# A selective-scan kernel: single PSUM banks for the decays, delta loaded one unit ahead, side stages at half the rate

## The chip, the cores and the metric

The kernel runs on one core of a Trainium2 chip. The metric is the device time in microseconds, the median of several runs of the whole program; lower is better. One further execution was recorded by the hardware profiler, and all views below are of it.

## What is computed

Four layers on an image batch `x` of shape (4, 64, 64, 96). Layers 2 and 3 are linear attention and a small quantised feed-forward network; the change does not touch them. Layers 0 and 1 are 2D selective scans ("SS2D"). Their core, cut:

```python
xz = einsum('bhwc,ec->bhwe', x, in_proj_w);  xx, z = split(xz, 2)         # 96 -> 2 x 192 channels
xc = silu(depthwise_conv3x3(xx) + conv_b)
xs = stack([x_hw, x_wh, x_hw[..., ::-1], x_wh[..., ::-1]])                # 4 directions k, L = 4096 steps
dts, Bmat, Cmat = split(einsum('bkdl,kcd->bkcl', xs, x_proj_weight), ...)  # 6, 16, 16 rows
delta = softplus(einsum('bkrl,kdr->bkdl', dts, dt_projs_weight) + bias)
h = exp(delta * A) * h + delta * B * u                                    # per step, state of 16 per channel
y = einsum('bken,bkn->bke', h, C)                                         # + D * u, directions added up
out = out_proj(layernorm(y) * silu(z))
```

## The kernel before, in words

The batch is cut into two pairs of images, and layers 0 and 1 give four *phases* (layer, pair), run one after the other. In a phase 8 groups (4 directions × 2 images) × 16 states fill the 128 partitions. The 4096 steps are cut into 8 chunks of 512, the 192 channels into 16 blocks of 12. A chunk and a block make a *unit*: 128 units a phase, 512 in all.

For each unit:
- `load` (L321) issues on SP's queue four loads of `dlt` (delta, 8 partitions each at 0, 32, 64 and 96) and four of `h` (delta·u, 8 groups spread over 128 partitions, 768 KB each). `h` has four buffers, `dlt` two.
- `times_b` (L339): four multiplications `h = h·b` on POOL.
- `scan` (L345), six times a unit (*slots*). A slot takes two channels: two replication matmuls on PE (L353, 8 rows of delta to 128 partitions, in the row group of that channel) into a tile `a` of two PSUM banks, two exponentials on ACT in place (L356), two scans on DVE (L360), which read `a` and overwrite `h`. The pool `p_a` has two such tiles, four banks. After the last slot ACT copies the final states to `carry` (L370).
- `contract` (L372), four times a unit, for the unit before: 32 small matmuls with the weights `cw` on PE (L381) into one bank of `p_y` (two banks), a copy to `d` on ACT (L391); after the fourth, four stores `y<-d` (L402). The weights are made on POOL once a chunk (`weights`, L301).

*Side stages* are generators whose `yield`s cut them into small steps. `prepare` (L131) makes `delta`, `du` and `bc` of the next phase: statistics, two convolutions (L228, one bank per chunk, nine matmuls and a silu), and `steps` (L250): per direction and chunk two x_proj matmuls (L257), a copy `xd` (L260), two dt_w matmuls (L267), two softplus (L273), a product on DVE (L276), and three stores. `finish` (L406) turns `y` of the phase before into the layer's output. They take PSUM banks from `bank()`, a pool `p_bg` of two.

The loop `run` (L557) mixes all this. For unit `at`, slot `n`, it calls `scan`, in slots 0 to 3 `contract` of unit `at-1`, in slot 4 `fetch` of unit `at+3` (loads and `times_b`), and then advances the side stages by `rate` 1.5 steps: nine a unit. When three units are left before the next phase, what is left of the side stages is run out. Before the first unit `prepare` of phase 0 runs alone; after the last, `finish` of phase 3; then layers 2 and 3.

The order of each engine's queue is settled at build time by a scheduler that starts from this program order and may move instructions by priority and by when it believes their inputs to be ready. All DMAs go through SP's queue in order; a DMA also waits until the one eight places ahead of it in that queue has landed.

Of the kernel before, what the change touches and what calls it, by code (L numbers as in the profile page):

```python
# [9 lines left out]
F32 = mybir.dt.float32  # L10
F16 = mybir.dt.float16
FP8 = mybir.dt.float8e5
AF = mybir.ActivationFunctionType
ALU = mybir.AluOpType
PSUM = bass.MemoryType.PSUM
# [6 lines left out]
C = 96  # L22
# [4 lines left out]
G = 2 * K  # L27
PAD = HW + 2
TC = 512
NC = L // TC  # L30
ROWS = TC // HW
EB = 12
NEB = E // EB
ER = EB // 4
XD = 2 * NS + R + 1
HID = 384
NF = HID // 128
EPS = 1e-5
LN_EXP = "natural_log_exp_and_others"
SQRT_HALF = 0.7071067811865476  # L40

# [33 lines left out]
class Consts:  # L75
    def __init__(self, nc, pool, a):
# [14 lines left out]
        self.eps = pool.tile([128, 1], F32, name="eps")  # L91
        nc.vector.memset(self.eps, EPS)


def neg_rsqrt(nc, cst, var, ln, r, sq):
# [3 lines left out]
    nc.scalar.activation(sq, r, AF.Square, scale=SQRT_HALF)  # L99
    nc.vector.scalar_tensor_tensor(sq, var, EPS, sq, ALU.add, ALU.mult)  # L100
    nc.vector.scalar_tensor_tensor(r, sq, 1.5, r, ALU.subtract, ALU.mult)
# [9 lines left out]
class Scans:  # L111
    def __init__(self, tc, ctx, cst, a):
        nc = self.nc = tc.nc
        self.tc, self.cst, self.a = tc, cst, a

        def pool(name, bufs, **space):
            return ctx.enter_context(tc.tile_pool(name=name, bufs=bufs, **space))

        self.dram = pool("stage", 2, space=DRAM)
        self.keep = pool("keep", 2)  # L120
        self.units = pool("units", 2)
        self.p_a = pool("p_a", 2, space=PSUM)
        self.p_y = pool("p_y", 2, space=PSUM)
        self.p_bg = pool("p_bg", 2, space=PSUM)

    def bank(self):
        return self.p_bg.tile([128, TC], F32, name="bg")

# [119 lines left out]
    def steps(self, ph, sp, xc, xp, dt_w, i, k, c):  # L250

        nc, cst = self.nc, self.cst
        g = 2 * k + i
        u = scan_view(xc, k, c)
        ps = self.bank()
        for h in range(2):
            nc.tensor.matmul(rows(ps[:XD]), xp[:, k, h], u[:, h], start=h == 0, stop=h == 1)  # L257
        xd = sp.tile([XD, TC], F32, name="xd")

        nc.scalar.activation(xd, ps[:XD], AF.Identity, bias=cst.one_row)  # L260
        yield
        nc.sync.dma_start(ph.bc[c][g], xd[: 2 * NS])
        delta = sp.tile([C, 2, TC], F32, name="dl")
        raw = []
        for m in range(2):
            ps = self.bank()
            nc.tensor.matmul(  # L267
                ps[:C], dt_w[2 * NS :, k, m * C : (m + 1) * C], xd[2 * NS :], start=True, stop=True
            )
            raw.append(ps)  # L270
        yield
        for m in range(2):
            nc.scalar.activation(delta[:, m], raw[m][:C], AF.Softplus)  # L273
        yield
        du = sp.tile([C, 2, TC], F32, name="du_sb")
        nc.vector.tensor_tensor(rows(du), rows(delta), u, ALU.mult)  # L276
        nc.sync.dma_start(ph.delta[c][g].rearrange("(h q) t -> q h t", h=2), delta)
        yield
        nc.sync.dma_start(ph.du[c][g].rearrange("(h q) t -> q h t", h=2), du)
# [37 lines left out]
    class Unit:  # L317
        def __init__(self, ph, c, eb):
            self.ph, self.c, self.eb = ph, c, eb

    def load(self, u):  # L321

        nc, ph = self.nc, u.ph
        h, v = divmod(u.eb, NEB // 2)
        u.first = [h * C + r * (C // 4) + ER * v for r in range(4)]
        u.dl = self.units.tile([128, ER, TC], F32, name="dlt")
        u.h = self.units.tile([128, EB, TC], F32, name="h", bufs=4)
        for r, at in enumerate(u.first):
            nc.sync.dma_start(u.dl[32 * r : 32 * r + G], ph.delta[u.c][:, at : at + ER])
        for r, at in enumerate(u.first):  # L330
            nc.sync.dma_start(
                u.h[:, ER * r : ER * r + ER].rearrange("p e t -> p (e t)"),
                ph.du[u.c][:, at : at + ER]
                .rearrange("g e t -> g (e t)")
                .unsqueeze(1)
                .broadcast_to([G, NS, ER * TC]),
            )
# [4 lines left out]
            h = u.h[:, ER * r : ER * r + ER]  # L342
            self.nc.gpsimd.tensor_tensor(h, h, b, ALU.mult)  # L343

    def scan(self, u, n):  # L345

        nc, ph = self.nc, u.ph
        half, i = divmod(n, ER)
        a = self.p_a.tile([128, 2, TC], F32, name="a")
        for j in range(2):  # L350
            r = 2 * half + j
            part = slice(32 * r, 32 * r + G)
            nc.tensor.matmul(a[:, j], self.cst.rep[part], u.dl[part, i], start=True, stop=True)  # L353
        for j in range(2):
            at = u.first[2 * half + j] + i
            nc.scalar.activation(a[:, j], a[:, j], AF.Exp, scale=ph.a_col[:, at : at + 1])  # L356
        for j in range(2):
            e = ER * (2 * half + j) + i
            at = u.eb * EB + e
            nc.vector.tensor_tensor_scan(  # L360
                u.h[:, e],
                a[:, j],
                u.h[:, e],
                0.0 if u.c == 0 else ph.carry[:, at : at + 1],
                ALU.mult,
                ALU.add,
            )
        if n == EB // 2 - 1 and u.c < NC - 1:
            at = u.eb * EB
            nc.scalar.copy(ph.carry[:, at : at + EB], u.h[:, :, TC - 1])  # L370

    def contract(self, u, l1):  # L372

        nc, ph = self.nc, u.ph
        y = self.p_y.tile([128, TC], F32, name="y_ps")
        for l2 in range(8):
            for j in range(4):  # L380
                nc.tensor.matmul(  # L381
                    view(y[32 * j : 32 * j + 32], l2 * EB, (8 * EB, 4), (1, EB)),
                    u.cw[l1][:, 8 * j + l2],
                    view(u.h, 64 * l1 + 16 * j + l2, (256, 2), (8, 2), (TC, EB)),
                    start=True,
                    stop=True,
                )
        if l1 == 0:

            u.d = self.units.tile([128, 4, 2, 4, 4 * EB], F32, name="d")  # L390
        nc.scalar.copy(  # L391
            u.d[:, :, :, l1], y[:, : 32 * EB].rearrange("p (t h x) -> p t h x", t=4, h=2)
        )
        if l1 < 3:
            return
        for t in range(4):
            b, m = divmod(t, 2)

            dst = ph.y[:, u.c * 8 : u.c * 8 + 8, u.eb, b].rearrange(
                "g (j m) h x -> m j g (h x)", m=2  # L400
            )[m]
            nc.sync.dma_start(dst, u.d[t::4, t].rearrange("p h l x -> p (h l x)"))  # L402
# [154 lines left out]
    def run(self, phases):  # L557

        def behind(p):
            if p > 0:
                yield from self.finish(phases[p - 1])
            if p + 1 < len(phases):
                yield from self.prepare(phases[p + 1])

        units = [
            self.Unit(ph, c, eb) for ph in phases for c in range(NC) for eb in range(NEB)
        ]
        per = NC * NEB  # L570
        slots = EB // 2

        def fetch(u):
            if u.eb == 0:
                self.start_chunk(u.ph, u.c)
            self.load(u)
            self.times_b(u)

        for _ in self.prepare(phases[0]):
            pass  # L580
        for u in units[:3]:
            fetch(u)
        self.weights(units[0].ph)
        rate = 1.5
        due = 0.0
        rest = iter(())
        for at, u in enumerate(units):
            for n in range(slots):
                self.scan(u, n)
                if n == 0:  # L590
                    u.cw = u.ph.cw if u.eb or at == 0 else None
                if at and n < 4:
                    self.contract(units[at - 1], n)
                if n == 4:
                    if at and u.eb == 0:
                        self.weights(u.ph)
                        u.cw = u.ph.cw
                    if at % per == 0:
                        rest = behind(at // per)
                        due = 0.0  # L600
                    if at + 3 < len(units):
                        if (at + 3) % per == 0:
                            for _ in rest:
                                pass
                        fetch(units[at + 3])
                due += rate
                while due >= 1.0:
                    next(rest, None)
                    due -= 1.0
        for q in range(4):  # L610
            self.contract(units[-1], q)
        for _ in self.finish(phases[-1]):
            pass

# [233 lines left out]
```

## Time and profile before

| | us |
|---|---|
| median of 3 runs (18317.12 to 18345.54) | 18334.98 |
| the profiled execution | 18288.92 |
| its span | 18287.0 |
| before the first scan (`prepare` of phase 0) | 852 |
| scans, four phases | 15494 |
| after the last scan (`finish` of phase 3) | 424 |
| layers 2 and 3 | 1517 |

| engine, over the span | busy us | share |
|---|---|---|
| PE (matmul) | 13227.8 | 72% |
| DVE | 9175.7 | 50% |
| POOL | 7455.9 | 41% |
| ACT | 7427.5 | 41% |

The four phases last 3771, 4095, 4091 and 3538 us. In the profile a row of a group gives busy time, mean duration and the idle time ahead of it with what ended it; `h<-du` reads "tile h, from du", and `xN` is a count. A fp32 matmul is two instructions in the trace.

### The profile page before, as it was taken

The numbers are of one execution on the slowest core, as the hardware profiler recorded it, in microseconds if no ns is written. First come the engines' busy times: TensorE is split into PE (matmuls) and PEld (weight loads), VectorE is DVE, ScalarE is ACT, GpSimd is POOL, SyncE is SP. The second block draws the span as 40 slices with busy tenths as digits, with TensorE's granted clock in tenths as the row PEclk, the third lists the DMA queues.
The fourth block names the chain that finished last, engine by engine and source line by source line (L and its number), as shares of the span: only waits on it lengthen the run. The fifth ranks groups of instructions, "written<-read, shape, count | busy, mean of one in ns | idle before, by whom it ended". The sixth has DMA issues, their size and how long they took to land. (4 is left out here: it accounts for less than half of the span.)

```text
span 18287.0 us, 356175 instructions
## 1 busy us (share of the span) xinstructions
PE 13227.8 (72%) x155712; PEld 6559.2 (36%) x155712; DVE 9175.7 (50%) x8726; ACT 7427.5 (41%) x12019; POOL 7455.9 (41%) x2572
## 2 busy tenths in 40 slices
PE   7887876666787897666787887666786666666555
PEld 2233333333453333333453333333453333335222
DVE  1144455555454545555454545555555555552333
ACT  2244443333333544333333544333334333342555
POOL 0034355555333435555333434555435555540000
PEclk6676666666667676666667676666666666666666
DMA  3345454444443545444443544444444444442000
GB/s 83 85 121 147 128 157 145 144 149 147 136 131 105 159 132 155 145 143 150 135 127 107 159 132 149 147 147 151 133 134 143 140 148 144 144 135 59 7 7 7
DMA packets 865414, 2293.37 MB, mean 125 GB/s; under 512 B 240854, under 2 KB 441688, under 8 KB 863476
## 3 DMA queue, kind: packets, MB, share of 16 engines
q1 hardware_dynamic: 863860, 2270.58, 42.2%
q8 instruction: 1228, 20.12, 0.5%
q14 instruction: 326, 2.67, 0.0%
HBM read 1907.51 MB, written 362.81 MB: 124 GB/s over the span
## 5 line engine op out<-in xcount | busy, mean ns | idle before, releaser
L343 POOL TENSOR_TENSOR h<-h,b 128x1536 f32<-128x1536 f32 x2048 | 7111.7, 3476 | 7564.1 <-DMA h<-du 6435.2
L360 DVE TENSOR_TENSOR_SCAN h<-a,carry,h 128x512 f32<-128x512 f32 x5376 | 6540.8, 1267 | 5372.2 <-ACT a L356 4189.9
L353 PE MATMUL a<-dlt,rep 8*128 8x512 f32 x12288 | 5474.3, 944 | 3072.7 <-DVE h L360 3054.1
L356 ACT ACTIVATE a<-a,a_col 128x512 f32<-128x512 f32 x6144 | 4013.6, 661 | 4628.3 <-PE a L353 4527.3
L381 PEld LDWEIGHTS y_ps<-h,cw 128*32 128x32 f32 x131072 | 2917.4, 146 | 3042.2 <-issue 2322.6
L381 PE MATMUL y_ps<-h,cw 128*32 128x48 f32 x131072 | 3274.1, 267 | 702.5 <-issue 353.2
L353 PEld LDWEIGHTS a<-dlt,rep 8*128 8x128 f32 x12288 | 1428.9, 258 | 4863.8 <-DVE h L360 4445.4
L391 ACT COPY d<-y_ps 128x384 f32<-128x384 f32 x2048 | 938.0, 481 | 1476.1 <-PE y_ps L381 1256.1
L360 DVE TENSOR_TENSOR_SCAN h<-a,h 128x512 f32<-128x512 f32 x768 | 892.2, 1208 | 1125.6 <-ACT a L356 705.3
L228 PE MATMUL bg<-xc,taps 96*96 96x512 f32 x2304 | 1013.4, 603 | 69.7 <-DVE xc L214 59.7
L267 PE MATMUL bg<-xd,dt_w 7*96 7x512 f32 x1024 | 859.9, 985 | 158.5 <-ACT xd L260 158.2
L276 DVE TENSOR_TENSOR du_sb<-dl,xc 96x1024 f32<-96x1024 f32 x256 | 473.7, 1850 | 878.0 <-ACT dl L273 869.2
L257 PE MATMUL bg<-xc,x_proj 96*39 96x512 f32 x1024 | 893.8, 1018 | 1.6 <-ACT dl L273 1.6
L309 POOL TENSOR_TENSOR cw<-c,gmask 128x256 f32<-128x256 f32 x512 | 323.8, 687 | 1345.2 <-DMA c<-bc 669.3
L454 PE MATMUL bg<-yk,perm 128*128 128x192 f32 x2048 | 623.4, 454 | 86.0 <-DMA yk<-y 85.6
L228 PEld LDWEIGHTS bg<-xc,taps 96*96 96x96 f32 x2304 | 380.3, 166 | 702.1 <-issue 649.2
L674 POOL MEMSET tn<- 1x4096 f32 x8 | 28.3, 3542 | 1409.3 <-PE pa L715 1386.1
L370 ACT COPY carry<-h 128x12 f32<-128x12 f32 x448 | 94.3, 210 | 1191.9 <-DVE h L360 998.3
L454 PEld LDWEIGHTS bg<-yk,perm 128*128 128x128 f32 x2048 | 473.4, 264 | 258.7 <-issue 144.8
L267 PEld LDWEIGHTS bg<-xd,dt_w 7*96 7x96 f32 x1024 | 224.1, 245 | 639.5 <-ACT xd L260 376.6
L260 ACT ACTIVATE xd<-bg,one_row 39x512 f32<-39x512 f32 x256 | 174.6, 682 | 575.3 <-PE bg L257 487.6
L235 ACT ACTIVATE xc<-bg,conv_b 96x512 f32<-96x512 f32 x128 | 87.2, 682 | 785.8 <-PE bg L228 785.8
(108 smaller groups left out, 6478.1 us busy)
## 6 DMA issues: line engine op xcount, KB each, us to landing
h<-du SPq DMA_DIRECT2D x2048, 768.0 KB
delta<-dl SPq DMA_DIRECT2D x256, 384.0 KB
du<-du_sb SPq DMA_DIRECT2D x256, 384.0 KB
dlt<-delta SPq DMA_DIRECT2D x2048, 48.0 KB
y<-d SPq DMA_DIRECT2D x2048, 48.0 KB
yk<-y SPq DMA_DIRECT2D x256, 384.0 KB
ud<-xu SPq DMA_DIRECT2D x128, 192.0 KB
ud_f<-ud SPq DMA_DIRECT2D x128, 192.0 KB
```

What stands on the lines that cost most here:

```text
L228: nc.tensor.matmul(rows(ps[:C]), taps[:, tap, h * C : (h + 1) * C], xn[:, ROWS * c + dy : ROWS * (c + 1) + dy, dx : dx + HW], start=tap == ...
L257: nc.tensor.matmul(rows(ps[:XD]), xp[:, k, h], u[:, h], start=h == 0, stop=h == 1)
L267: nc.tensor.matmul(ps[:C], dt_w[2 * NS :, k, m * C : (m + 1) * C], xd[2 * NS :], start=True, stop=True)
L276: nc.vector.tensor_tensor(rows(du), rows(delta), u, ALU.mult)
L309: self.nc.gpsimd.tensor_tensor(view(cw, t, (256, 4), (32, 8), (4, G)), view(ph.c_next, 256 * b + 64 * l1 + 8 * m, (16, 4), (1, 8), (0, G)) ...
L343: self.nc.gpsimd.tensor_tensor(h, h, b, ALU.mult)
L353: nc.tensor.matmul(a[:, j], self.cst.rep[part], u.dl[part, i], start=True, stop=True)
L356: nc.scalar.activation(a[:, j], a[:, j], AF.Exp, scale=ph.a_col[:, at : at + 1])
L360: nc.vector.tensor_tensor_scan(u.h[:, e], a[:, j], u.h[:, e], 0.0 if u.c == 0 else ph.carry[:, at : at + 1], ALU.mult, ALU.add,)
L381: nc.tensor.matmul(view(y[32 * j : 32 * j + 32], l2 * EB, (8 * EB, 4), (1, EB)), u.cw[l1][:, 8 * j + l2], view(u.h, 64 * l1 + 16 * j + l2, ...
L391: nc.scalar.copy(u.d[:, :, :, l1], y[:, : 32 * EB].rearrange("p (t h x) -> p t h x", t=4, h=2))
L454: nc.tensor.matmul(ps[:, : 4 * n].rearrange("p (w v e) -> p w v e", w=4, v=nv), cst.perm[:, k], view(t, off, (sw if k < 2 else -sw, 4), (1 ...
```

## The change

Four things:
1. The pools. `p_a` becomes six single banks, one decay (one channel) each. `p_y` and `p_bg` become one pool `p_m` of two banks, which contraction and side stages share. Outside the scans `bank()` takes from the six.
2. `scan` takes four channels (one of each row group) at a time: four replications, four exponentials, four scans; three times a unit in place of six.
3. The loads of `dlt` leave `load` for `load_delta`, called for unit `at+1` after the first step of unit `at`. `contract` is called twice in each of the first two steps, `fetch` in the second.
4. RATE stays 1.5 per step of the loop, which has three steps a unit: 4.5 side steps a unit. `steps` has a softplus right after each dt_w matmul and a `yield` after each.

```diff
-        self.p_a = pool("p_a", 2, space=PSUM)
-        self.p_y = pool("p_y", 2, space=PSUM)
-        self.p_bg = pool("p_bg", 2, space=PSUM)
+        self.p_a = pool("p_a", 6, space=PSUM)
+        self.p_m = pool("p_m", 2, space=PSUM)
+        self.scanning = False
     def bank(self):
-        return self.p_bg.tile([128, TC], F32, name="bg")
+        if self.scanning:
+            return self.p_m.tile([128, TC], F32, name="m")
+        return self.p_a.tile([128, TC], F32, name="a")
...
         for m in range(2):
             ps = self.bank()
             nc.tensor.matmul(ps[:C], dt_w[...], xd[2 * NS :], start=True, stop=True)
-            raw.append(ps)
-        yield
-        for m in range(2):
-            nc.scalar.activation(delta[:, m], raw[m][:C], AF.Softplus)
-        yield
+            nc.scalar.activation(delta[:, m], ps[:C], AF.Softplus)
+            yield
...
+    def load_delta(self, u):
+        nc, ph = self.nc, u.ph
         u.dl = self.units.tile([128, ER, TC], F32, name="dlt")
         for r, at in enumerate(u.first):
             nc.sync.dma_start(u.dl[32 * r : 32 * r + G], ph.delta[u.c][:, at : at + ER])
...
-    def scan(self, u, n):
-        half, i = divmod(n, ER)
-        a = self.p_a.tile([128, 2, TC], F32, name="a")
-        for j in range(2):
-            r = 2 * half + j
+    def scan(self, u, i):
+        decay = []
+        for r in range(4):
+            a = self.p_a.tile([128, TC], F32, name="a")
             part = slice(32 * r, 32 * r + G)
-            nc.tensor.matmul(a[:, j], self.cst.rep[part], u.dl[part, i], start=True, stop=True)
+            nc.tensor.matmul(a, self.cst.rep[part], u.dl[part, i], start=True, stop=True)
+            decay.append(a)
...
-        y = self.p_y.tile([128, TC], F32, name="y_ps")
+        y = self.p_m.tile([128, TC], F32, name="m")
...
-            for n in range(slots):
-                self.scan(u, n)
-                if n == 0:
-                    u.cw = u.ph.cw if u.eb or at == 0 else None
-                if at and n < 4:
-                    self.contract(units[at - 1], n)
-                if n == 4:
+            for i in range(ER):
+                self.scan(u, i)
+                if i == 0 and at + 1 < len(units):
+                    self.load_delta(units[at + 1])
+                if at and i < 2:
+                    self.contract(units[at - 1], 2 * i)
+                    self.contract(units[at - 1], 2 * i + 1)
+                if i == 1:
...
                         fetch(units[at + 3])
-                due += rate
+                due += RATE
```

More of the change, by code (lines that the diff above doesn't have):

```diff
@@ L38 @@
 EPS = 1e-5
+RATE = 1.5
 LN_EXP = "natural_log_exp_and_others"
@@ L263, in steps @@
         delta = sp.tile([C, 2, TC], F32, name="dl")
-        raw = []
         for m in range(2):
@@ L319, in __init__ @@
             self.ph, self.c, self.eb = ph, c, eb
+            h, v = divmod(eb, NEB // 2)
+            self.first = [h * C + r * (C // 4) + ER * v for r in range(4)]
+    def load_delta(self, u):
+        nc, ph = self.nc, u.ph
+        u.dl = self.units.tile([128, ER, TC], F32, name="dlt")
+        for r, at in enumerate(u.first):
+            nc.sync.dma_start(u.dl[32 * r : 32 * r + G], ph.delta[u.c][:, at : at + ER])
     def load(self, u):
         nc, ph = self.nc, u.ph
-        h, v = divmod(u.eb, NEB // 2)
-        u.first = [h * C + r * (C // 4) + ER * v for r in range(4)]
-        u.dl = self.units.tile([128, ER, TC], F32, name="dlt")
         u.h = self.units.tile([128, EB, TC], F32, name="h", bufs=4)
-        for r, at in enumerate(u.first):
-            nc.sync.dma_start(u.dl[32 * r : 32 * r + G], ph.delta[u.c][:, at : at + ER])
         for r, at in enumerate(u.first):
@@ L343, in times_b @@
             self.nc.gpsimd.tensor_tensor(h, h, b, ALU.mult)
-    def scan(self, u, n):
+    def scan(self, u, i):
         nc, ph = self.nc, u.ph
-        half, i = divmod(n, ER)
-        a = self.p_a.tile([128, 2, TC], F32, name="a")
-        for j in range(2):
-            r = 2 * half + j
+        decay = []
+        for r in range(4):
+            a = self.p_a.tile([128, TC], F32, name="a")
             part = slice(32 * r, 32 * r + G)
[L353 to L358, printed above, removed]
+            nc.tensor.matmul(a, self.cst.rep[part], u.dl[part, i], start=True, stop=True)
+            decay.append(a)
+        for r, a in enumerate(decay):
+            at = u.first[r] + i
+            nc.scalar.activation(a, a, AF.Exp, scale=ph.a_col[:, at : at + 1])
+        for r, a in enumerate(decay):
+            e = ER * r + i
             at = u.eb * EB + e
@@ L361, in scan @@
                 u.h[:, e],
-                a[:, j],
+                a,
                 u.h[:, e],
@@ L367, in scan @@
             )
-        if n == EB // 2 - 1 and u.c < NC - 1:
+        if i == ER - 1 and u.c < NC - 1:
             at = u.eb * EB
@@ L570, in run @@
         per = NC * NEB
-        slots = EB // 2
         def fetch(u):
@@ L582, in run @@
             fetch(u)
+        self.load_delta(units[0])
         self.weights(units[0].ph)
-        rate = 1.5
+        self.scanning = True
+        rest = iter(())
         due = 0.0
-        rest = iter(())
         for at, u in enumerate(units):
-            for n in range(slots):
-                self.scan(u, n)
-                if n == 0:
-                    u.cw = u.ph.cw if u.eb or at == 0 else None
-                if at and n < 4:
-                    self.contract(units[at - 1], n)
-                if n == 4:
+            if u.eb or at == 0:
+                u.cw = u.ph.cw
+            for i in range(ER):
[6 more added lines that the diff above has]
+                if i == 1:
                     if at and u.eb == 0:
@@ L599, in run @@
                         rest = behind(at // per)
-                        due = 0.0
                     if at + 3 < len(units):
@@ L611, in run @@
             self.contract(units[-1], q)
+        self.scanning = False
         for _ in self.finish(phases[-1]):
```

## The prediction

> **What bounds the kernel now.** I read the page first (busy shares, slices), then the stretches by stage, then the waits and the order of time inside one unit. A unit is 12 scans on DVE; 512 units follow each other in four phases of 128. The row of stretches, restricted to the scan line L360, gives the pace:
>
> ```profile
> 4623.00:7135.00 2512.00, 927.13 (x768) 0.68 0.47 134
> 7135.00:8718.00 1583.00, 932.35 (x769) 0.62 0.48 147
> ```
>
> Both halves of phase 1 hold 768 scans, 64 units. The first, with side work (`finish` of the phase before, `prepare` of the next), takes 2512/64 = 39.3 us a unit, the second, without any, 1583/64 = 24.7 us. The same stretches over all engines:
>
> ```profile
> 4623.00:7135.00 2512.00, 2024.46 (x20488) 1011.46 (x20488) 1224.49 (x1162) 1078.51 (x1681) 943.19 (x321) 0.68 0.47 134
> 7135.00:8718.00 1583.00, 1060.39 (x17920) 542.39 (x17920) 932.35 (x769) 613.90 (x1072) 918.94 (x321) 0.62 0.48 147
> ```
>
> With side work PE is busy 2024 of 2512 us (81%): PE bound. Without it PE, DVE and POOL are all near 60%, and the waits of the free half name the transfer:
>
> ```profile
> POOL h L343 <- DMA h<-du: 550.8, 215, 8.6
> ```
>
> In the order of time POOL's four multiplications of a unit each start when a piece of `h` lands:
>
> ```profile
> 7804.04 3.42 POOL L343 TENSOR_TENSOR h<-h,b 128x1536 f32<-128x1536 f32 x1 [6.74 <-DMA h<-du]
> ...
> 7810.13 3.47 POOL L343 TENSOR_TENSOR h<-h,b 128x1536 f32<-128x1536 f32 x1 [2.67 <-DMA h<-du]
> ...
> 7816.32 3.42 POOL L343 TENSOR_TENSOR h<-h,b 128x1536 f32<-128x1536 f32 x1 [2.72 <-DMA h<-du]
> ```
>
> A piece every 6.1 us; four pieces are the 24.7 us. So a free unit is bound by its 3 MB of `h`, a unit with side work by PE.
>
> [...] the share stays at 0.48 of 16, 7.7 engines, in every free stretch, so the transfer is saturated though it looks half idle. [...]
>
> ```profile
> 7809.77 2.08 PE L353 MATMUL a<-dlt,rep 8*128 8x512 f32 x4
> ...
> 7811.78 1.62 PE L381 MATMUL y_ps<-h,cw 128*32 128x48 f32 x64
> ...
> 7815.80 3.25 PE L353 MATMUL a<-dlt,rep 8*128 8x512 f32 x8 [2.40 <-DVE h L360]
> ```
>
> Each replication is two instructions: a pair takes 2.08 us and the contraction behind it starts 2.01 us after it. [...] The trace shows the 1283, and the activation 1.29 us after the load began[...]. I use 1.28.
>
> **The change part by part.**
>
> *Delta one unit ahead.* The load of `dlt` for three units ahead waits in SP's queue until the replications two units before it are through (L329, 16.67 us across its four issues at 7803.94), with the `h` loads behind it. That wait goes. But the transfer is saturated, so what is late next is the same 3 MB: worth 0 to 0.6 us a unit; I take 0. Same DMAs, same number.
>
> *Single banks.* A scan starts after one exponential instead of two: in the trace exponentials start at 7801.82 and the scan at 7803.21, 1.39 us; one exponential is 0.66 us. It shortens the ring, which isn't what bounds a free unit.
>
> *The order on PE.* This decides, and the diff doesn't show it. In the built order of before, each unit has its four contraction groups placed between replications, so they run while DVE scans. In the built order of after, a free unit is: contraction of unit u (first one waits for DVE, the last scan of u), then the replications of u+1: one alone ahead of the last contraction matmul, three, two, then six that each wait for a scan, then the contraction of u+1. So four replications are rarely side by side, and contraction and scans take turns. A free unit on this chain: 4 × 1.61 (contraction) + 2.0 (lone replication) + 2.1 (the next) + 0.66 (exponential) + 0.3 (handing over) + 11 × 1.21 (the scans left; four take 4.81) = 24.4 us. Beside it the transfer has 24.7. Two limits this close: I take 25.2. 147 such units × 0.5 = +74 us.
>
> *Side stages spread.* The steps due fall from 9 to 4.5 a unit. `finish` has 200 steps, the statistics 11, the two convolutions 80, the projections (`steps`) 256: 547 in phases 1 and 2, 347 in phase 0, 200 in phase 3. Divided by 4.5 that is 44.4, 2.4, 17.8 and 56.9 units. The total work is the same, so it gains only if it runs beside the scans. PE has about six scans of free time, 7.3 us, after a unit's last replication; but in the order of after most projection work stands behind the contraction that waits for the last scan.
> - Projections: 3.5 us of L257 and 3.4 of L267 a step (893.8/256 and 859.9/256), × 1.125 steps = 7.7 us a unit, of which the order puts some 1.7 ahead of the contraction. Up to the fourth replication: 6.4 + 6.0 + three lone replications at 2.0 + 2.1 = 20.5; exponential 0.7; nine scans left 10.9; in most units a softplus stands between exponentials, 1.28 + 0.59 + 1.28 = 3.2. That is 35.3; dt_w beside a replication (they use different rows, and overlap at 2326 us) takes about 1 off, waits not listed may add as much. I take 35, bounds 31 and 38.
> - `finish`: 16 groups of 4 × 0.61 + 4 × 0.335 = 3.8 us and two slices of 14 us per quarter. Two groups fit under the scans; the shared pair of banks allows no more, since the copy of `carry`, which waits for the last scan, is ahead of their evacuation on ACT. A unit full of groups: 15 + 2.9 + 6.4 + 18 − 7.5 = 34.8; slices (4.3 us of PE a unit): about 27. Weighted 20 to 30: 30 us, bounds 28 and 33.
> - Convolutions: 16 chunks of 7.9 us per half, 4.5 to a unit: 3.55 units of about 55, the rest near 27: 338 us per half. Statistics 26 a unit.
>
> *Table loads.* Softplus is now one per step: the order has 1208 loads against 823, +385 × 1.28 = 494 us of ACT, not all on the path; what is, stands in the 3.2 above.
>
> *Shared pair of banks* for contraction and side work: PE waits for copies of 0.48; inside the above, 0 to 1 us a unit.
>
> *Outside the phases*, `bank()` has six banks: PE is busy 703 of 852 us before the scans and 325 of 424 after; I take −40 us (0 to −100).
>
> Sum. Phases 1 and 2: 44.4 × 30 + 62 + 676 + 56.9 × 35 + 6.5 × 25.2 = 4226 each, against 4095: +131. Phase 0: 62 + 676 + 1992 + 50.9 × 25.2 = 4013 against 3771: +242. Phase 3: 1332 + 83.6 × 25.2 = 3439 against 3538: −99. Together +405, less 40: +365. The profiled execution is 18288.9 us (span 18287.0), so 18654; the median of the runs is 46 higher: 18700.
>
> **The rivals.**
> - *Side work disappears under the transfer* (faster). For it: PE would need only 16.6 + 8.2 us in a unit of the first half now spread over two, DVE 15. Then a unit with side work costs 24.7 plus its own DMA, some 29 us: phases 3684 twice, 3531, 3330, a sum of 14229 against 15495, 17070 in all. Halfway (projections 31, `finish` 28) it is 17750. Against: the order above.
> - *The turns cost more* (slower still): softplus twice in a unit's scans[...]: 39 and 33 us, + 171 × 4 + 133 × 3 = +1083: 19780. It would decide as soon as the projections pass 37 us a unit.
> - *It cancels*: projections at 33, with the rest as above: 171 × 2 = 342 less, 18360.
> - *The change doesn't act*: four replications don't stand together in the order, and the lead of `dlt` is hidden by the saturated transfer; that part is likely, and only the spreading acts.
>
> **How the numbers follow.** Turns as summed 0.57, turns costing more 0.18, cancelling 0.06, side work hidden at least half 0.19. A measurement of this kernel can tell about 0.2% (37 us). Slower 0.75, same 0.06, faster 0.19. The range takes the bounds of projections and `finish` (171 × −4 and 133 × −2 one way, 171 × 3 and 133 × 3 the other, not all at once): 18100 to 19400.
>
> **What would show it.** In the profile after: free stretches near 25 us a unit (about 1600 us for 64); DVE idle ahead of its scans for some 10 us at a time, once a unit, and L384 waiting for DVE; projections at 35 a unit; about 1208 table loads; the wait of POOL for `h` shorter in side stretches. Wrong it would be if units with side work run at 29 to 31 us with the DMA share at 0.48 or above throughout: then the order doesn't bind and the transfer does.

## The result, and the profile after

The changed kernel takes 18553.58 us (median of 4 runs, 18520.44 to 18619.85), the kernel before 18326.05 in the same session: a ratio of 1.013, with a 95% interval from 1.0098 to 1.0161. It is slower by 1.3%. The profiled execution has a span of 18518.7 us, 231.7 more than before.

The page of the changed kernel, its groups of instructions (busy time, mean ns of one, idle time ahead of the engine and what ended it; the lines have moved: the scan is L363 now, the contraction L384, the multiplication by b L346):

```profile
PE 13016.6 (70%) x155712; PEld 6734.7 (36%) x155712; DVE 9278.6 (50%) x8726; ACT 7835.8 (42%) x12404; POOL 7465.1 (40%) x2572
...
L346 POOL TENSOR_TENSOR h<-h,b 128x1536 f32<-128x1536 f32 x2048 | 7121.1, 3479 | 8143.3 <-DMA h<-du 6610.6
L363 DVE TENSOR_TENSOR_SCAN h<-a,carry,h 128x512 f32<-128x512 f32 x5376 | 6461.6, 1263 | 5041.0 <-issue 2599.0
...
L384 PE MATMUL m<-h,cw 128*32 128x48 f32 x131072 | 3281.9, 267 | 2291.1 <-issue 983.8
...
L457 PE MATMUL m<-yk,perm 128*128 128x192 f32 x1536 | 421.2, 417 | 825.5 <-DMA yk<-y 823.4
```

The rows of the scan and of the first matmul of `finish` in the kernel before:

```profile
L360 DVE TENSOR_TENSOR_SCAN h<-a,carry,h 128x512 f32<-128x512 f32 x5376 | 6540.8, 1267 | 5372.2 <-ACT a L356 4189.9
L454 PE MATMUL bg<-yk,perm 128*128 128x192 f32 x2048 | 623.4, 454 | 86.0 <-DMA yk<-y 85.6
```

The work is the same (the last `finish` has a row of its own now, hence 1536 for 2048); what differs is the waiting. Before, the idle time of the scans ended mostly with an exponential (4189.9 us of 5372.2). Now its largest part has the releaser "issue": the scan had nothing left to wait for that the profile shows, and the order of time below shows what stands ahead of it. The other new number is the 823.4 us in which PE stands at the first matmul of `finish` for `yk`, which was 85.6.

Three stretches, restricted to the scan line (start and end, length, DVE busy and number of scans, granted clock, DMA share, GB/s): `finish` and projections of phase 1, the free units of phase 3.

```profile
4641.00:6126.00 1485.00, 624.84 (x528) 0.68 0.46 132
6564.00:7447.00 883.00, 405.75 (x336) 0.63 0.48 149
14504.00:16612.00 2108.00, 1202.42 (x1008) 0.62 0.48 142
```

With 12 scans a unit these are 33.8 us for a unit with `finish`, 31.5 with projections, 25.1 free. The phases last 3721, 4175, 4154 and 3642 us (before 3771, 4095, 4091, 3538): −50, +80, +63 and +104. Up to the first scan pass 920 us (852), after the last 1907 (1941). The sum, 197 + 68 − 34, is the 231.

One free unit in the order of time (start, duration, engine, line, and in brackets the idle time ahead with its releaser):

```profile
15200.88 2.46 PE L384 MATMUL m<-h,cw 128*32 128x48 f32 x103 [0.16 <-issue]
...
15203.27 1.12 PE L355 MATMUL a<-dlt,rep 8*128 8x512 f32 x2
...
15204.59 10.01 PE L355 MATMUL a<-dlt,rep 8*128 8x512 f32 x22
...
15205.18 14.35 DVE L363 TENSOR_TENSOR_SCAN h<-a,carry,h 128x512 f32<-128x512 f32 x12 [8.16 <-issue]
...
15219.67 3.02 PE L384 MATMUL m<-h,cw 128*32 128x48 f32 x127 [5.07 <-DVE h L363]
```

The contraction of one unit, one replication, all the others, twelve scans in one run, and only then the next contraction, which waited 5.07 us for the last of them. DVE had been idle 8.16 us ahead of its run. Contraction and scans take turns, as the built order had it.

### The profile page after: what moved, and what is told of

Its sections match the earlier page's. It is cut to its first block, busy times and chain, and to the rows that moved or that the text cites. A ratio compares the mean times of both kernels' runs of the same rounds, so it can differ in the third digit from the quotient of the medians.

```text
span 18518.7 us, 353643 instructions
## 1 busy us (share of the span) xinstructions
PE 13016.6 (70%) x155712; PEld 6734.7 (36%) x155712; DVE 9278.6 (50%) x8726; ACT 7835.8 (42%) x12404; POOL 7465.1 (40%) x2572
## 3 DMA queue, kind: packets, MB, share of 16 engines
HBM read 1907.51 MB, written 362.81 MB: 123 GB/s over the span
## 5 line engine op out<-in xcount | busy, mean ns | idle before, releaser
L346 POOL TENSOR_TENSOR h<-h,b 128x1536 f32<-128x1536 f32 x2048 | 7121.1, 3479 | 8143.3 <-DMA h<-du 6610.6
L363 DVE TENSOR_TENSOR_SCAN h<-a,carry,h 128x512 f32<-128x512 f32 x5376 | 6461.6, 1263 | 5041.0 <-issue 2599.0
L384 PE MATMUL m<-h,cw 128*32 128x48 f32 x131072 | 3281.9, 267 | 2291.1 <-issue 983.8
L384 PEld LDWEIGHTS m<-h,cw 128*32 128x32 f32 x131072 | 2939.0, 140 | 3864.1 <-issue 3043.2
L355 PEld LDWEIGHTS a<-dlt,rep 8*128 8x128 f32 x12288 | 1814.5, 250 | 3273.6 <-DVE h L363 1892.3
L394 ACT COPY d<-m 128x384 f32<-128x384 f32 x2048 | 983.3, 484 | 2058.5 <-PE m L384 1891.3
L363 DVE TENSOR_TENSOR_SCAN h<-a,h 128x512 f32<-128x512 f32 x768 | 878.8, 1203 | 1148.7 <-issue 753.2
L457 PE MATMUL m<-yk,perm 128*128 128x192 f32 x1536 | 421.2, 417 | 825.5 <-DMA yk<-y 823.4
L231 PE MATMUL m<-xc,taps 96*96 96x512 f32 x1728 | 789.4, 615 | 103.4 <-issue 67.1
L457 PEld LDWEIGHTS m<-yk,perm 128*128 128x128 f32 x1536 | 311.5, 237 | 947.1 <-issue 667.5
L269 PE MATMUL m<-xd,dt_w 7*96 7x512 f32 x768 | 559.4, 835 | 127.6 <-ACT xd L263 98.9
L260 PE MATMUL m<-xc,x_proj 96*39 96x512 f32 x768 | 594.6, 894 | 0.3 <-issue 0.2
L359 ACT ACT_TABLE_LOAD x431 | 553.0, 1283 | 55.3 <-PE a L355 47.7
L231 PEld LDWEIGHTS m<-xc,taps 96*96 96x96 f32 x1728 | 285.5, 168 | 595.7 <-issue 526.4
L272 ACT ACT_TABLE_LOAD x301 | 386.2, 1283 | 8.9 <-DMA delta<-dl 3.7
```

The source lines that it names most:

```text
L231: nc.tensor.matmul(rows(ps[:C]), taps[:, tap, h * C : (h + 1) * C], xn[:, ROWS * c + dy : ROWS * (c + 1) + dy, dx : dx + HW], start=tap == ...
L269: nc.tensor.matmul(ps[:C], dt_w[2 * NS :, k, m * C : (m + 1) * C], xd[2 * NS :], start=True, stop=True)
L272: nc.scalar.activation(delta[:, m], ps[:C], AF.Softplus)
L355: nc.tensor.matmul(a, self.cst.rep[part], u.dl[part, i], start=True, stop=True)
L359: nc.scalar.activation(a, a, AF.Exp, scale=ph.a_col[:, at : at + 1])
L363: nc.vector.tensor_tensor_scan(u.h[:, e], a, u.h[:, e], 0.0 if u.c == 0 else ph.carry[:, at : at + 1], ALU.mult, ALU.add,)
```

## The experiments

All times are medians; the ratio is to the kernel before in the same session (18314.76 us for the first four, 18254.04 for the next four, 18297.65 and 18282.34 later), with its 95% interval.

| kernel | us | ratio | table loads on ACT |
|---|---|---|---|
| before | 18254 to 18326, by session | 1 | 823 |
| changed kernel | 18554 | 1.013 (1.0098 to 1.0161) | 1208 |
| 1: changed, delta loaded in `fetch` | 18167 | 0.9912 (0.9889 to 0.9936) | 873 |
| 2: before, delta one unit ahead | 19753 | 1.0779 (1.0759 to 1.0799) | 866 |
| 3: before, rate 0.75 | 18240 | 0.9962 (0.995 to 0.9973) | 919 |
| 4: changed, rate 3 | 18504 | 1.0092 (1.0059 to 1.0124) | 930 |
| 5: before, `h` on 16 engines | 21088 | 1.1551 (1.1534 to 1.1568) | |
| 6: changed, `h` on 16 engines | 22473 | 1.2307 (1.2288 to 1.2325) | |
| 7: changed, softplus in pairs | 18301 | 1.0036 (1.0009 to 1.0063) | 1156 |
| 8: 1 with `h` on 16 engines | 21863 | 1.1976 (1.1958 to 1.1994) | |
| 9: before, two copies of `du` | 18421 | 1.0073 (1.0054 to 1.0093) | 817 |
| 10: 1 and 7 together | 18151 | 0.9929 (0.9906 to 0.9952) | 857 |
| 11: before, padded rows of `du` | 18270 | 0.9988 (0.9973 to 1.0002) | |
| 12: 10 with two copies of `du` | 17529 | 0.9591 (0.9573 to 0.961) | 857 |

### 1 and 2: the lead of delta

Run 1 takes the lead of `dlt` out of the changed kernel: it is loaded in `fetch` again, ahead of `h`, three units before its use.

```diff
         def fetch(u):
...
+            self.load_delta(u)
             self.load(u)
...
-        self.load_delta(units[0])
...
-                if i == 0 and at + 1 < len(units):
-                    self.load_delta(units[at + 1])
```

> The changed kernel with the delta load put back beside the h load, three units ahead (two buffers, so its wait for the replications is back). In the built order the contraction of a unit then stands ahead of the fourth replication of the next in 0 to 0.5 of its matmuls instead of 0.3 to 1.0. Theory A, PE's order makes contraction and scans take turns: side units fall from about 32 to 28-30 us, free units stay at 24.5, in all 17900 to 18200. Theory B, the 8-engine transfer of h sets all units: no change, 18450 to 18600. Theory C, what costs is PE standing at L457 for the yk loads: no change either, the yk waits stay near 820 us.

Run 2 does that part alone: the kernel before, where after the first scan call of a unit the `dlt` of the next is loaded.

```diff
-    def load(self, u):
+    def load_delta(self, u):
...
+        self.load_delta(units[0])
...
+                if n == 0 and at + 1 < len(units):
+                    self.load_delta(units[at + 1])
```

> The kernel before with the delta load alone moved, one unit ahead after slot 0. In the built order the contraction's share ahead of the fourth replication rises from 0.25 to 0.5-0.94. Theory A: slower than before, free units 25 to 26.5 us, side units 40 to 43, in all 18500 to 18800. Theory B: the same or up to 0.5% faster, since SP is no longer held at the delta load, 18230 to 18340. Theory C: as before, 18330.

The lead alone costs 1438 us, far more than the 500 expected; without it the changed kernel is 387 us faster (18167 against 18554), and faster than the kernel before, inside theory A's time. The order on PE says why. Counted in the traces, the share of a unit's contraction that runs ahead of the fourth replication of the next unit is, in free units, 0.25 in the kernel before, 0.95 with the lead alone, 1 in the changed kernel and 0.5 in run 1. In the changed kernel it is also 1 in most units with projections, but 0.13 (median) in those with `finish` of phase 1: the turns stand in the free units and in those with projections. The edit moves only the place of the load in the program; that the scheduler then believes the replications ready at another time is the explanation that fits, and wasn't looked into. The waits of the scans over the whole program (us, times, longest), first the changed kernel:

```profile
DVE h L363 <- issue: 3352.2, 314, 43.4
DVE h L363 <- ACT a L359: 2151.7, 827, 52.1
...
DVE h L363 <- POOL h L346: 582.9, 74, 23.6
```

then run 1:

```profile
DVE h L363 <- POOL h L346: 3798.2, 915, 30.0
DVE h L363 <- ACT a L359: 2562.4, 507, 141.5
...
DVE h L363 <- issue: 185.9, 52, 13.3
...
PE m L457 <- DMA yk<-y: 56.7, 36, 3.8
```

The turns are gone ("issue" falls from 3352 to 186, PE's wait for `yk` from 823 to 57), and the `h` that POOL delivers takes their place: 583 to 3798. So a unit with projections falls from 31.1 to 27.8 us on average, while one with `finish` (34.3 for 33.8) and a free one (24.9 to 25.2 for 23.9 to 25.1) gain nothing: there the next wait lies just behind the one removed. In run 2 the turns are there without the four replications in a row, and a free unit takes 28.4 to 28.9 us where it took 24.5 to 25.2:

```profile
DVE h L363 <- issue: 3993.0, 393, 24.1
...
PE y_ps L384 <- DVE h L363: 1694.5, 433, 11.0
```

A rival is that `dlt` itself arrives too late for the replications when it is loaded so late. The waits of the replications for that DMA, in the changed kernel and in run 2, speak against it:

```profile
PE a L355 <- DMA dlt<-delta: 565.2, 102, 46.2
```

```profile
PE a L356 <- DMA dlt<-delta: 61.1, 8, 44.0
```

In run 2 they are 61 us beside 1438 lost. In the changed kernel 565 us (136 in run 1) aren't nothing, but only 22 of them lie in the two stretches with projections of phase 1, where run 1 gains some 3 us a unit. What the rest adds to the 387 us wasn't separated.

Part of a later beginning goes with the lead too. The first scan comes at 919 us in run 2, 920 in the changed kernel and 918 in run 7, which have it; at 852 in the kernel before and 849 in run 3, and at 885 and 886 in runs 1 and 10, which do not. Why a load placed there delays it, and why runs 1 and 10 are still later than the kernel before, was not tried.

### 3 and 4: spreading the side stages

Run 3 is the kernel before with one edit, run 4 the changed kernel with one.

```diff
-        rate = 1.5
+        rate = 0.75
```

> The kernel before with the side steps alone spread, 4.5 a unit instead of 9; the order keeps 0.25 of the contraction ahead of the fourth replication. Theory A: side work hides beside the scans, side units 28 to 31 us, in all 17500 to 18000. Theory B: 29 us by the transfer, 17100 to 17300. Theory C: finish units stay at 33 or more because of waits for yk, all others near 29, in all about 17600.

```diff
-RATE = 1.5
+RATE = 3.0
```

> The changed kernel with 9 side steps a unit as before, so spreading alone undone. Theory A: with the turns kept, side units of 40 to 48 us over half as many units, in all 18800 to 19100. Theory B: the transfer idles again in side units, free units 24.7, in all 18700 to 18900. Theory C: the same number of waits for yk, 18450 to 18600.

Run 3 gains 0.4%, less than any of the three expectations had. Its four phases last 3770, 4088, 4095 and 3534 us, within 7 us of the kernel before each, though in phase 1, for one, 22 units with `finish` at 41.0 us became 44 at 31.9. In the kernel before, the half of phase 1 that had the side work is dearer by 2512 − 64 × 24.7 = 931 us than 64 free units, and PE is busier in it by 2024 − 1060 = 964 us. The two nearly agree, as if every microsecond of PE that side work needs lengthened the unit it is in; then spread over twice as many units it adds half as much to each. That PE is the cause is not shown by this: in run 12 below the side stretches get shorter with the same work on PE.

The rate in the changed kernel is as indifferent: 18504 against 18554, intervals that overlap. The time is inside theory C's, though PE's wait for `yk` fell from 823 to 547 us. With twice the rate, 22 units with `finish` take 42 us instead of 44 taking 34. Run 3 also has the changed kernel's rate, so 18554 against 18240 is what banks, grouping, lead and split softplus cost together.

### 7 and 10: the softplus in pairs

Run 7 undoes the split of the softplus in the program of the changed kernel.

```diff
+        raw = []
...
-            nc.scalar.activation(delta[:, m], ps[:C], AF.Softplus)
-            yield
+            raw.append(ps)
+        yield
+        for m in range(2):
+            nc.scalar.activation(delta[:, m], raw[m][:C], AF.Softplus)
+        yield
```

> The changed kernel with the two softplus of a projection step run one after the other as before, so that the 385 table loads that the change added go. Theory A (the prediction: the loads cost ScalarE 494 us that lie in part on the scans' path): 18250 to 18500 us. Theory B (they lie in ScalarE's idle time): within 60 us of 18554.

It gains 0.9% over the changed kernel, inside theory A's time, but not by the way expected: only 52 of the 385 additional table loads go (1208 to 1156). The rows of the loads ahead of exponentials and softplus, in the changed kernel:

```profile
L359 ACT ACT_TABLE_LOAD x431 | 553.0, 1283 | 55.3 <-PE a L355 47.7
L272 ACT ACT_TABLE_LOAD x301 | 386.2, 1283 | 8.9 <-DMA delta<-dl 3.7
```

in run 7:

```profile
L363 ACT ACT_TABLE_LOAD x405 | 519.6, 1283 | 51.9 <-PE a L359 44.6
L276 ACT ACT_TABLE_LOAD x275 | 352.8, 1283 | 10.8 <-DMA delta<-dl 6.0
```

and in run 1, which keeps the split:

```profile
L359 ACT ACT_TABLE_LOAD x270 | 346.4, 1283 | 4.9
L272 ACT ACT_TABLE_LOAD x202 | 259.2, 1283 | 4.2 <-DMA delta<-dl 0.6
```

Most of the loads came with the order that the lead of `dlt` makes in the changed kernel. In the traces 107 of the 192 pairs of softplus in the phases have exponentials between the two in the changed kernel, 8 in run 1, none in the kernel before. In run 7 there are still 81: the scheduler keeps the pair apart though the program has it together, so this run doesn't show what the table loads cost. The lead isn't enough for them either: run 2 has the turns with no pair apart and 866 loads, and run 4, with twice the rate, has 22 pairs apart and 930 loads at nearly the changed kernel's time. Run 10 joins both edits.

> The changed kernel with both edits that gained: delta loaded in the fetch, and the two softplus of a step side by side again. Theory A (the two gains add: 0.8% below the kernel before and 0.9% below the changed kernel): 17900 to 18070 us. Theory B (the second gain was made of table loads and waits that the first edit removes already, since with it there are 873 loads and not 1208): 18100 to 18220 us.

18151 against 18167 is no difference, so the gains do not add, as theory B has it. Of the 227 us between the profiled executions of the changed kernel and run 7, 122 lie in phase 3, which has no projections, so part of its gain belongs to the order that the edit happened to give there; that is not explained further.

### 5, 6 and 8: h on 16 engines

The prediction had a free unit bound by the transfer of `h` on 8 engines. The 8 are an estimate: the share of 0.48 of 16 is 7.7, and in the packet records of the free stretch of phase 3 eight packets of `h` are under way at once for 70.5% of the time, more for 7.4%. In these runs each DMA carries one group, 16 partitions, in the expectation that 16 engines take part.

```diff
-        for r, at in enumerate(u.first):
+        for g in range(G):
+            src = ph.du[u.c][g, u.first[0] : u.first[0] + 1]
             nc.sync.dma_start(
-                u.h[:, ER * r : ER * r + ER].rearrange("p e t -> p (e t)"),
-                ph.du[u.c][:, at : at + ER]
-                .rearrange("g e t -> g (e t)")
-                .unsqueeze(1)
-                .broadcast_to([G, NS, ER * TC]),
+                u.h[NS * g : NS * g + NS].rearrange("p (r e) t -> p r (e t)", r=4),
+                bass.AP(src.tensor, src.offset, [[0, NS], [C // 4 * TC, 4], [1, ER * TC]]),
             )
```

> The kernel before, with the h tiles loaded by eight DMAs of one group each, so that 16 DMA engines carry each of them and not 8. Nothing else changes. Theory A (the prediction: the free stretches are bound by the transfer of h on 8 engines, at a DMA share of 0.48): free units fall from 24.7 us to 18 to 21 us (PE is busy some 18 of them), side units stay at 39, where PE is behind; with some 150 free units that is 600 to 1000 us less: 17300 to 17750 us. Theory B (the order on PE is what bounds the free units too): free units stay within 0.7 us of 24.7 and the time within 100 us of 18315. Theory C (the memory side is the limit and not the number of engines): the DMA share rises above 0.6 with the same GB/s and the time stays within 1%.

> The changed kernel with the same h loads on 16 engines. Theory A (in the changed kernel the turns, contraction behind the last scan and replications behind the contraction, are a second chain of some 24 us that stands as soon as the transfer is gone): free units stay at 23.5 to 25.5 us, and the time within 250 us of 18554. Theory B (the transfer alone holds the free units): they fall to 18 to 21 us and the time to 17500 to 17950 us.

> The changed kernel with delta loaded in the fetch, three units ahead (the edit that gave 18167), and h on 16 engines. Theory A (the delta lead sets the order and the transfer the free units, two separate bounds): free units 18 to 21 us, 17200 to 17650 us, faster than both kernels. Theory B (with the transfer gone the turns or PE hold the free units at 24): 18000 to 18200 us.

All three lose 15 to 23%, and none of the theories had that. The DMA queue in the free stretch of phase 3 (packets, MB, share of 16 engines) is, in the kernel before,

```profile
q1 hardware_dynamic: 65915, 299.40, 47.7%
```

and in run 5:

```profile
q1 hardware_dynamic: 75465, 298.91, 92.1%
```

The share of 16 engines is 92.1% for 47.7%, more than 8 of them could give, for the same bytes, and in more time: a free unit takes 30.4 us. From the packet records of the free units of phase 3, packets of 6144 bytes, the rows of `h`, counted from the first of them to the last:

| | mean of a packet, ns | time without such a packet under way | free unit, us |
|---|---|---|---|
| before | 334 | 1.5% | 25.2 |
| 5 (16 engines, one row at a time) | 797 | 1.2% | 30.4 |
| 9 (16 engines, a row for each) | 452 | 28.5% | 24.7 |
| 11 (8 engines, padded rows) | 331 | 1.5% | 25.1 |
| 12 (10 with a row for each) | 451 | 25.4% | 23.9 |

### 9 and 11: a row for each engine

In run 5 the 16 partitions of a group, one DMA, are copies of one row. That all the engines read this row at the same time was not shown: a packet record names neither engine nor address. Run 9 stores `du` twice and keeps the loads as they were, over 16 rows of the source instead of 8.

```diff
-        ph.du = [self.dram.tile([G, E, TC], F32, name="du", bufs=2 * NC) for _ in range(NC)]
+        ph.du = [self.dram.tile([2 * G, E, TC], F32, name="du", bufs=2 * NC) for _ in range(NC)]
...
-        nc.sync.dma_start(ph.du[c][g].rearrange("(h q) t -> q h t", h=2), du)
+        for k in range(2):
+            nc.sync.dma_start(ph.du[c][2 * g + k].rearrange("(h q) t -> q h t", h=2), du)
...
-                .broadcast_to([G, NS, ER * TC]),
+                .broadcast_to([2 * G, NS // 2, ER * TC]),
```

> The kernel before, with du stored twice in DRAM, so that the h loads go out on 16 engines of which each reads rows of its own (in the run with one group a DMA all 16 read one row at the same time, and a packet of 6144 B took 797 ns where it takes 333 ns before). It adds 98 MB of stores. Theory A (it was the common row that slowed the packets): packets stay under 400 ns, free units fall from 24.7 us to 18 to 21 us, 17300 to 17900 us. Theory B (what one core draws is capped near 130 GB/s, however many engines and rows): packets go to 600 to 800 ns, free units stay at 24 us or above, 18300 us or more.

Run 11 pads the rows of a group.

```diff
-        ph.du = [self.dram.tile([G, E, TC], F32, name="du", bufs=2 * NC) for _ in range(NC)]
+        ph.du = [self.dram.tile([G, E + 1, TC], F32, name="du", bufs=2 * NC) for _ in range(NC)]
...
-        nc.sync.dma_start(ph.du[c][g].rearrange("(h q) t -> q h t", h=2), du)
+        nc.sync.dma_start(ph.du[c][g, :E].rearrange("(h q) t -> q h t", h=2), du)
```

> The kernel before, with one row more in each group of du in DRAM, so that the rows that the 8 engines read together are no longer exactly 384 KB apart. Nothing else changes. Theory A (the 8 rows meet in the same part of the memory, which is why a packet takes 333 ns where the quickest take 234): packets fall to 240 to 290 ns, free units to 18 to 22 us, 17400 to 18100 us. Theory B (the distance has no part in it): within 60 us of the kernel before.

The distance of the rows has no part in it (331 ns against 334, no difference in time). Run 9 is the one that decides on the prediction's premise. With rows of their own the packets take 452 ns, and the transfer of `h` is done in less time: 28.5% of the free stretch has no packet of `h` under way. Yet a free unit still takes 24.7 us (before: 25.2 in the same phase, 24.7 in phase 1). That is theory B's time but not its reason: packets stayed well under its 600 ns, and the engines had time to spare. One thousand microseconds of it over all engines (PE, PEld, DVE, ACT and POOL busy, clock, DMA share, GB/s), first the kernel before, then run 9:

```profile
15000.00:16000.00 1000.00, 663.90 (x11202) 338.61 (x11200) 582.67 (x480) 384.97 (x679) 578.06 (x208) 0.62 0.48 144
```

```profile
15000.00:16000.00 1000.00, 665.95 (x11368) 344.47 (x11360) 591.53 (x488) 389.60 (x691) 578.95 (x196) 0.61 0.66 146
```

The same number of scans (480 and 488) at the same GB/s (144 and 146): the transfer follows the pace and does not set it. The scans' waits in the free stretch of the kernel before (2116 us) say so too, and could have been read there:

```profile
DVE h L360 <- ACT a L356: 681.9, 261, 9.7
PE a L353 <- DVE h L360: 595.3, 268, 10.6
...
DVE h L360 <- POOL h L343: 114.3, 43, 10.8
```

Scans wait for exponentials and replications for scans: the loop of the decays through two pairs of banks. For `h` they wait 114 us, 5%. POOL waits 741.9 us for its DMA there and yet seldom holds up a scan: it works ahead of them. That this loop sets the 24.7 us is read from the waits; no run changed the banks alone.

### 12: several limits loosened together

In run 10 the same view of its free stretch (2056 us, scan at L367) has `h` in the first place:

```profile
DVE h L367 <- POOL h L350: 553.4, 192, 12.0
...
DVE h L367 <- ACT a L363: 272.8, 75, 10.8
```

so there the two copies should act. Run 12 is run 10 with the three edits of run 9.

> The changed kernel with delta loaded in the fetch, the softplus pair side by side, and du stored twice so that h comes over 16 engines with a row of its own for each. In the kernel before the two copies changed nothing in the free stretches: there scans wait for exponentials and PE (DVE waits for h 2% of the time). In the version with the first two edits scans wait for POOL and so for h 27% of the free time. Theory A (two limits of nearly the same size: the decay loop in the kernel before, the transfer as soon as single banks have loosened that loop; with both loosened PE, busy some 17.5 us a unit, is next): free units fall from 24.5 to 18 to 21 us; with some 147 of them, 500 to 950 us below 18151: 17200 to 17650 us, faster than both kernels. Theory B (the decay loop on PE, ScalarE and VectorE holds 24 us in this version too): 18100 to 18350 us, and DVE waits for ScalarE in h's place.

17529 us, 4.1% below the kernel before and the fastest of all; what cost 0.7% in run 9 gains 3.4% here. The time is inside theory A's, the place is not. A free unit takes 23.9 us, not 18 to 21: its scans now wait for exponentials (free stretch, 2006 us, scan at L368):

```profile
DVE h L368 <- ACT a L364: 578.4, 84, 11.0
...
DVE h L368 <- POOL h L351: 113.0, 25, 14.9
```

which is the half of theory B that came true. Most of the gain lies in the side stretches. Against run 10 the phases are shorter by 41, 227, 217 and 179 us. The 44 units with `finish` of phase 1 took 1494 us and take 1360, 30.9 each; in them DVE's wait for POOL falls, from run 10 to run 12:

```profile
DVE h L367 <- POOL h L350: 550.4, 97, 28.4
```

```profile
DVE h L368 <- POOL h L351: 357.1, 56, 23.8
```

What is left there is still a wait for `h`, ahead of the wait for exponentials.

## Why the prediction came out as it did

The sign and the range held, and the time is off by 0.8% of the whole (18700 for 18554). The sum was +365 on the profiled execution, measured +231. That it came so close is in part luck, since its terms erred in opposite directions: phase 0 was given +242 and had −50, phase 3 was given −99 and had +104. What the prediction had right is the order of turns on PE, and that it makes the changed kernel the slower one.

- *A free unit is bound by its 3 MB of h*: wrong for the kernel before (run 9). The reading stopped at POOL's wait for the DMA, and a share of 0.48, taken for 8 engines nearly always busy, looked like the proof. Nor do the pieces come evenly: the three shown start 6.1 to 6.2 us apart, the fourth of that unit 4.1 us after the third. What these runs show of the number of engines is the share: 0.48 of 16 with the 8 groups outermost in the source, 0.66 with 16 rows there (run 9), 0.92 with the 16 partitions of one group a DMA (run 5). In the kernel before only 1.5% of the free stretch of phase 3 has no packet of `h` under way. What does not follow is that a transfer so seldom idle sets the pace. What would have told it was one step further in the same view: who waits for POOL.
- *Delta one unit ahead, worth 0*: this step failed. The lead is what makes the order of turns (runs 1 and 2), and costs 1438 us alone and 387 inside the change. The prediction took the turns from the built order and counted them, so its total did not miss them, but it put them down to no part of the change, and called this one hidden.
- *Single banks, nothing*: not tried alone. With two copies of `du` a free unit takes 24.7 us with pairs (run 9) and 23.9 with single banks (run 12), and under turns the changed kernel is 1199 us faster than run 2; single banks with four replications together, the paired or split softplus and the rate are mixed in both, and what four together save on PE over two pairs was not shown.
- *Free units, 25.2*: 23.9 to 25.1. The chain of turns is seen in the trace; its terms add up to 24.8 and not to the 24.4 written. That there are two limits close together was right as well: with the turns removed, the scans wait most for `h` at 24.9 to 25.2 (run 1), and with that loosened for the decays, at 23.9 in phase 3 (run 12).
- *Projections, 35*: 31.1 on average, over 171 units the term mis-sized most. The 3.2 us for softplus between exponentials is one of its parts; how much of it is real is not shown. Run 7, which brings only some of the pairs together, has 30.2 on average.
- *`finish`, 30*: 33.6 to 34.9, the miss the other way. The sum counted PE and not the transfer. In phase 1's `finish` PE stands for `yk` 263 us, 6.0 a unit:

```profile
PE m L457 <- DMA yk<-y: 263.3, 24, 23.8
```

  That wait alone is not the 4 us missing: run 1 has removed it and stays at 34.3, since the scans then wait for `h`. Among the variants of the changed kernel only run 12, where both come faster, reaches 31. The kernel before at the same rate has 31.9 (run 3), so the changes other than the rate cost some 2 us here; which of them, was not taken apart.
- *Convolutions, 338 a half*: 348 and 336 in phase 1.
- *Table loads, 1208*: right in number, and 1283 ns each as in the rows above; wrong in cause: the split of softplus in the program accounts for 52 of the additional 385 (run 7); the lead at this rate brings most of the rest (873 loads in run 1, 930 in run 4).
- *Outside the phases, −40*: +34. Six banks for `bank()` did not shorten the beginning; the lead of `dlt` comes with a first scan about 35 to 70 us later.
- *Side work disappears under the transfer*: it does not. The sizes of that rival rested on the transfer as the bound (and its 8.2 us of PE a unit are 7.5 by the two stretches shown); run 3 shows that spreading alone gives 0.4%.

## What to carry over

A wait says that its engine had nothing to do, not that anything was late: before a resource is called the bound, follow the chain to the engine that ends last and ask whether it waited for the one named. Where a scheduler fixes the order of an engine's instructions, the place of a load is also an instruction to the scheduler; moving a small DMA cost 8% here, and the order that it makes has to be compared before its lead is valued. Where several limits lie within a microsecond of each other, loosening one gives nothing, or a loss, until the others are loosened too: run 9 lost 0.7% (with 100.7 MB of additional stores, 463.47 MB written for 362.81), the same edit with the same stores gained 3.4% in run 12.

## What was not expected of the hardware

The transfer of `h` became slower though the share of the DMA engines in use rose from 47.7% to 92.1% of 16. With one group a DMA, all copies of one row (run 5), a packet of 6144 bytes took 797 ns, with 16 rows of the source (run 9) 452, with 8 (the kernel before) 334; the quickest 5% take 234 or less there. Per microsecond the free stretches moved 132 KB of `h` in the kernel before and 109 in run 5. That the common row is the cause is the likeliest reading of run 9 against run 5; these also differ in the number of DMAs (four of 768 KB, eight of 384 KB) and in the order of their pieces, and that was not taken apart.
